# A graph network of two layers on one core: epsilon and offset of the layer norms and the mask of unlinked nodes go to VectorE, and every operation gets a new place

## The chip, the core and the metric

The kernel runs on one core of a Trainium2 chip. A core has five engines that each work through their own queue in order: TensorE (PE) for matrix products, VectorE (DVE), ScalarE (ACT), GpSimd (POOL), and SyncE (SP), which here only issues transfers between HBM and the on-chip memory SBUF. Products land in banks of a second on-chip memory, PSUM. The metric is device time in microseconds (us) of one execution, the median of several.

## The reference, cut to what matters

The input is 64 graphs of 256 nodes with 256 features each, and for each graph a 256 x 256 matrix `adj` of links, here 0 or 1. Two layers follow each other:

```python
# layer 0: attention with 8 heads of 32 features; values differ by the kind of link
attn = softmax(q @ k.T / sqrt(32))                      # q = x@Wq+bq, k = x@Wk+bk, per head
out  = sum_r (attn * (adj == r)) @ (x @ Wv[r] + bv[r])  # with links 0 and 1: r = 0, 1
x    = ln(x + out @ Wo + bo, g1, beta1)                 # norm 1
x    = ln(x + gelu(x @ W1 + b1) @ W2 + b2, g2, beta2)   # norm 2; 256 -> 1024 -> 256
# layer 1: two graph-attention steps, then a second feed-forward
def gat(h, W, a):
    Wh = h @ W
    e  = leaky_relu(Wh @ a[:256] + (Wh @ a[256:]).T, 0.2)
    return softmax(where(adj > 0, e, -9e15), axis=1) @ Wh
h = ln(x + gat(gat(x, W1, a1), W2, a2), g_ln1, b_ln1)            # norm 3
h = ln(h + relu(h @ w_ff1 + b_ff1) @ w_ff2 + b_ff2, g_ln2, b_ln2)  # norm 4
# ln(x) = (x - mean) * rsqrt(var + 1e-5) * g + b
```

So each graph has four layer norms, and the mask of the unlinked nodes is used twice, once in each graph-attention step.

## The kernel before, in words

`binary_graphs` writes one program for all 64 graphs. (A second function, `any_graphs`, serves links above 1; with this input it does no work.) Of a graph, the 256 nodes are two blocks of 128 partitions. All arithmetic is float32 except the links, which are bfloat16 once they have been transposed (`adT`).

**The stages of a graph, with the names of their operations.** The letters and digits stand for themselves below: a name like `bc1` is one operation of the plan.

- *Front.* `load` brings features and links, `cast` (GpSimd) makes the links bfloat16 and their transpose follows by a transfer, `xT` (VectorE) transposes the features, `xS` (GpSimd) makes sums of their blocks. `no` (L552) makes the mask of unlinked nodes from `adT`: 1 where a link is <= 0, 128x512, as unsigned bytes, on GpSimd.
- *Attention.* Two halves m = 0, 1 of four heads: `qk` (L558) and its copy `qkc`; the scores `s` (L606), whose matmuls use tiles of 32 rows; then per head VectorE's `max`, ScalarE's `exp`, VectorE's `rec` (the reciprocal of the sums), ScalarE's `nrm`, VectorE's `eT` (a transpose within squares of 32), a write to DRAM and a read back (`eW`, `eR`) that finish the transpose, and VectorE's `pm` (L638), the masked copy. `vp1` to `vp7` (L582) are the seven products of the values, for both kinds of link at once, `va` (L591) and `vb` their sums. `po` (L653) is the sum over both masks, with output tiles of 32 columns; ScalarE's `oT` (L659) copies it, `wo` (L673) projects it, `ya` adds the residual.
- *Feed-forward, twice* (prefix `a` and `b` in names; `ffa`, `ffb` in the rows): `T`, `W`, `R` transpose the input through DRAM, `t1` to `t4` (GpSimd) make differences of its blocks, `p1` to `p7` (L455) are the seven products of the way up, in the order 1, 2, 6, 7, 5, 4, 3 or near it, where 1, 6, 7 and 4 are accumulated in one and the same PSUM bank: between them ScalarE's copies `c1`, `c6`, `c7`, `c4` (L466) take the intermediate state out, and the next product waits for that copy. `a1`, `a7`, `a6` (VectorE, L472) add two further banks. `x0` to `x3` are the activation, `S1` to `S4` (GpSimd, L492) differences, `d1` to `d7` (L503) the seven products of the way down, `e` the additions to the residual.
- *Graph attention*: `ga` and `gac`; for steps A and B `ip`, `z`, `zl`, the masking `zm` (L708, VectorE's predicated copy of -9e15 where `no` is nonzero), `zx`, `ze`, `zd`; `h1` and `h1c`; `h2` (L745) and `h2a`.
- *Norm n of 1 to 4* (class `Norm`): `st` (VectorE: mean and variance, into `mv`), `rt` (GpSimd, L387 and L388: variance plus epsilon, then the power -1/2, into `rs`), `nb` (GpSimd, L392 and L393: mean times `rs`, then times -1), `ln` (ScalarE, L398, two instructions that apply scale `rs` and offset `nb`). After norms 2 and 4 GpSimd multiplies the gain (`lg`) and adds the shift (`lb`).

**What sets the order.** Nothing is reordered by a compiler. A table `PLACES` gives each of these operations a place in time; the operation of graph g is sorted by `g * PERIOD + place`, with a `PERIOD` of 46.802, and all operations of all graphs are written in that order. Since a graph's places spread over more than six periods, some six graphs are in flight, and between two projections `wo` on TensorE stand products of several graphs. An engine's own queue is that order, cut down to its instructions. An instruction waits for its inputs by semaphores, and everything behind it in its queue waits with it.

Four kinds of things come once and are sorted in by places of their own: 49 late loads of weights (`LOAD_PLACES`, issued by SyncE, L864), and the preparations of the values' weights, the output bias, the two feed-forwards and the graph attention (`V_PLACE`, `OUT_PLACE`, `FFA_PLACE`, `FFB_PLACE`, `GAT_PLACE`). Some first loads and graph 0's input stand ahead of everything.

**Orders that the change touches.** The queues of one period, from one projection to the next, as the places of the kernel before sort them:

```
TensorE: wo vp7 s0 qk1 vp2 bp1 bp2 bp6 vp5 vp3 bp7 bp5 bp4 bp3 ga1 ga0 s1 vp4 ipA bd1 ap1 ap2 bd5 ap6 ...
         ... bd4 bd3 po0 ad3 ad5 ad7 ad1 ad2 ad4 h2 vp1 ad6 qk0 vp6 po1
ScalarE: ln2 nrm13 nrm10 ln4 nrm11 exp02 qkc1 bc1 ln1 bc6 exp01 bc7 ... exp10 nrm01 nrm12 te ln3 qkc0 oT1
```

Rings of buffers: three PSUM banks for most products (`mm`), one bank for each of the four heads' scores, one for `po`; three buffers for `no`, six for each small tensor of the norms.

## Time and profile before

| | us |
|---|---|
| median of three runs | 3115.67 (3115.14 to 3116.3) |
| profiled execution, whole | 3118.7 |
| its span, first to last instruction | 3116.9 |
| mean granted TensorE clock | 0.987 of full speed |
| GpSimd, power of the norms, L388 | 713 ns, 256 times |
| ScalarE, application of the norms, L398 | 595 ns, 256 times |
| VectorE, reciprocal of the heads' sums, L624 | 149 ns a piece from 1000 to 2872 us |
| VectorE, masked copy `pm`, L638 | 899 ns, 512 times |

The profile comes from one execution with its own time, so durations are read against the span of that execution and not against the median. A row of a group gives the line of the kernel, the engine, the operation, the output and inputs by their names and shapes, how often it ran, its summed and mean time, and the idle time of the engine just ahead of it with the instruction that ended it. In timelines a row is the start, the length, the engine and the line, and several instructions of one kind in a row are one row. TensorE's lengths overlap a little, because matmuls are pipelined: a start is surer than an end.

### The profile page before, as it was taken

To read this page: it belongs to the slowest core of one execution; us is meant where nothing else is said; L and a number is where in the kernel's file an instruction comes from. 1 tells how busy PE (TensorE), PEld (TensorE's weight loads), DVE (VectorE), ACT (ScalarE), POOL (GpSimd) and SP (SyncE) were. 2 spreads that over 40 slices of the span, in tenths; PEclk is the share of its full clock that TensorE was granted. 3 is DMA by queue.
4 is the path that set the end of the run, shared out by engine and by line. 5 is a ranking of instruction groups with operands and counts; after the bars stand their busy time and mean duration, and the time that the engine had idled before them with its cause. 6 is when DMAs were issued, how large, how long until landed. Compare 5 with 4: busy or idle time off the path is not lost.

```text
span 3116.9 us, 72178 instructions
## 1 busy us (share of the span) xinstructions
PE 3020.8 (97%) x24797; PEld 2611.0 (84%) x24797; DVE 2618.7 (84%) x5545; ACT 2597.0 (83%) x7109; POOL 2364.2 (76%) x3142
## 2 busy tenths in 40 slices
PE   6899999999999999999999999999999999999985
PEld 4688888888888888888888888888888888888874
DVE  6888888888888888888888888888888888888852
ACT  5688888888888888888888888888888888888852
POOL 1577777877877877877877877877878777787763
PEclk8899999999999999999999999999999999999997
DMA  7554555455455455455455455455455555445410
GB/s 188 163 158 144 145 162 151 144 160 152 142 157 161 136 160 161 137 157 155 135 160 156 140 156 154 142 154 158 145 147 159 146 146 162 147 143 162 143 50 27
DMA packets 808371, 457.16 MB, mean 147 GB/s; under 512 B 334529, under 2 KB 717377, under 8 KB 808001
## 3 DMA queue, kind: packets, MB, share of 16 engines
q1 hardware_dynamic: 808000, 452.49, 50.3%
q8 instruction: 200, 3.28, 0.5%
q14 instruction: 171, 1.39, 0.1%
HBM read 242.63 MB, written 201.33 MB: 142 GB/s over the span
## 4 chain that ended last, share of the span: by engine, by line
PE 93%; DMA 2%; DVE 2%; ACT 2%; POOL 1%; issue 1%; SPq 0%; POOLq 0%; DVEq 0%; ACTq 0%
PE ffb_ps L455 14%; PE ffa_ps L455 13%; PE ffb_po L503 7%; PE po L653 7%; PE qk_ps L558 7%; PE ffa_po L503 7%; PE v_ps L582 6%; PE ffa_pq L503 6%; PE ffb_pq L503 5%; PE s L606 4%; PE wo_ps L673 4%; PE h_ps L730 4%; PE h_ps L745 3%; PE ga_wps L683 3%; DMA ffa_T<-ffa_T_d 1%
## 5 line engine op out<-in xcount | busy, mean ns | idle before, releaser
L619 ACT ACTIVATE e<-s,nmax 128x256 f32<-128x256 f32 x1024 | 473.6, 476 | 10.6 <-DVE nmax L611 10.4
L629 ACT ACTIVATE e<-e,rden 128x256 f32<-128x256 f32 x1024 | 447.6, 502 | 25.0 <-DVE rden L624 25.0
L638 DVE TENSOR_TENSOR pm<-eT,adT 128x512 f32<-128x512 f32 x512 | 449.5, 899 | 0.0
L340 DVE STREAM_TRANSPOSE eT_sq<-e 128x512 f32<-128x512 f32 x512 | 349.1, 691 | 7.3 <-ACT e L629 6.0
L611 DVE TENSOR_REDUCE nmax<-s 128x2 f32<-128x512 f32 x512 | 341.7, 669 | 2.0 <-PE s L606 2.0
L478 ACT ACTIVATE ffb_h<-ffb_h,bf_c 128x256 f32<-128x256 f32 x512 | 224.9, 503 | 49.0 <-DVE ffb_h L472 49.0
L492 POOL TENSOR_TENSOR ffb_t<-ffb_h 128x512 f32<-128x512 f32 x64 | 81.5, 1273 | 225.8 <-ACT ffb_h L478 225.8
L466 ACT COPY ffb_h<-ffb_ps 128x512 f32<-128x512 f32 x256 | 151.0, 590 | 99.6 <-PE ffb_ps L455 99.5
L472 DVE TENSOR_TENSOR ffb_h<-ffb_ps,ffb_h 128x512 f32<-128x512 f32 x192 | 132.8, 692 | 107.2 <-PE ffb_ps L455 104.2
L466 ACT COPY ffa_h<-ffa_ps 128x512 f32<-128x512 f32 x256 | 148.3, 579 | 83.5 <-PE ffa_ps L455 47.8
L492 POOL TENSOR_TENSOR ffa_t<-ffa_h 128x512 f32<-128x512 f32 x64 | 82.5, 1289 | 172.6 <-PE ffb_pq L503 155.0
L619 ACT ACTIVATION_READ_ACCUMULATOR e<-s,nmax 128x1 f32 x1024 | 211.5, 207 | 0.0
L478 ACT ACTIVATE ffa_h<-ffa_h,b_c 128x256 f32<-128x256 f32 x512 | 211.1, 506 | 0.1
L472 DVE TENSOR_TENSOR ffa_h<-ffa_ps,ffa_h 128x512 f32<-128x512 f32 x192 | 132.3, 689 | 79.7 <-ACT ffa_h L466 45.8
L388 POOL TENSOR_TENSOR rs_x<-rs_x,nhalf 128x2 f32<-128x2 f32 x256 | 182.5, 713 | 21.3
L492 POOL TENSOR_TENSOR ffb_t<-ffb_h,ffb_t 128x512 f32<-128x512 f32 x128 | 163.6, 1278 | 36.3 <-ACT ffb_h L478 35.6
L492 POOL TENSOR_TENSOR ffa_t<-ffa_h,ffa_t 128x512 f32<-128x512 f32 x128 | 185.0, 1445 | 5.0
L591 DVE TENSOR_TENSOR v<-v,v_ps 128x256 f32<-128x256 f32 x448 | 177.2, 407 | 2.0 <-PE v_ps L582 1.1
L398 ACT ACTIVATE ffa_res<-ffa_res,nb_x,rs_x 128x256 f32<-128x256 f32 x256 | 139.9, 595 | 25.2 <-POOL nb_x L393 24.8
L455 PE MATMUL ffb_ps<-ffb_T,f 128*128 128x128 f32 x1024 | 130.7, 283 | 26.7 <-DMA ffb_T<-ffb_T_d 22.9
L606 PE MATMUL s<-kT,qT 32*128 32x256 f32 x2048 | 149.8, 407 | 7.0 <-ACT e L619 6.0
L558 PE MATMUL qk_ps<-xT,wq 128*128 128x256 f32 x512 | 141.1, 399 | 15.9 <-DVE xT L529 8.4
(192 smaller groups left out, 9799.1 us busy)
## 6 DMA issues: line engine op xcount, KB each, us to landing
eT_d<-eT_sq SPq DMA_DIRECT2D x512, 256.0 KB, 3.1
eT<-eT_d SPq DMA_DIRECT2D x512, 256.0 KB, 3.6
xin<-in_x_dram SPq DMA_DIRECT2D x256, 64.0 KB, 3.6
adi<-in_adj_dram SPq DMA_DIRECT2D x64, 256.0 KB, 2.6
y<-in_x_dram SPq DMA_DIRECT2D x64, 256.0 KB, 2.9
ffa_T_d<-ffa_T_sq SPq DMA_DIRECT2D x64, 256.0 KB, 2.8
ffa_T<-ffa_T_d SPq DMA_DIRECT2D x64, 256.0 KB, 2.9
hT_d<-hT_sq SPq DMA_DIRECT2D x64, 256.0 KB, 2.1
```

Of the source, the lines that this page charges most:

```text
L340: nc.vector.transpose(self.sq.rearrange("p a c k y -> p (c k) a y"), src.rearrange("p c (k a x) -> p (c k) a x", k=KD, a=A))
L455: nc.tensor.matmul(self.ps[bank][:, f], w[:, f * P:(f + 1) * P], b, start=(i in (1, 2, 5) and f == 0), stop=(f == KF // 2 - 1), skip_group ...
L466: nc.scalar.copy(self.half_of(*{1: (0, 0), 6: (0, 1), 7: (1, 1), 4: (1, 0)}[i]), self.ps[0])
L478: nc.scalar.activation(h, h, self.func, bias=self.ba[:, f0 + f:f0 + f + 1])
L492: nc.gpsimd.tensor_tensor(out, a, b, ALU.subtract)
L503: nc.tensor.matmul(self.p[bank][:, k], a[:, f], seven[self.name[:3]][i][:, f], start=(f == 0), stop=(f == KF // 2 - 1))
L558: nc.tensor.matmul(p[:, i, :], w[:, k, m * P:(m + 1) * P], self.xT[:, k, :], start=(k == 0), stop=(k == KD - 1))
L606: nc.tensor.matmul(self.s4[m][h][:, ic * N:(ic + 1) * N], self.qT[hp, m, ic * P:(ic + 1) * P], self.kT[hp, m, :], start=True, stop=True)
L611: nc.vector.tensor_reduce(self.nmax[m, h], self.s4[m][h].rearrange("p (c n) -> p c n", c=C), AX.X, ALU.max, negate=True)
L619: nc.scalar.activation(e[:, ic, :], self.s4[m][h][:, ic * N:(ic + 1) * N], AF.Exp, bias=self.nmax[m, h][:, ic:ic + 1], accum_out=self.den[ ...
L629: nc.scalar.activation(e[:, ic, :], e[:, ic, :], AF.Copy, scale=self.rden[m, h][:, ic:ic + 1])
L638: nc.vector.tensor_tensor(self.pm[m, h].rearrange("p c k (b y) -> p (c k) b y", b=A), t.rearrange("p b c k y -> p (c k) b y"), self.adT.re ...
```

## The change

Three pieces of code differ, and the table of places as a whole.

1. In the norms, the addition of epsilon becomes an operation of its own, `ep`, made by VectorE; `rt` keeps only the power on GpSimd. The offset `nb`, two GpSimd instructions before, becomes a single VectorE instruction that computes (mean * -1) * `rs`. There are so four new operations `ep1` to `ep4` in the plan.
2. The mask `no` is made by VectorE, and as bfloat16 (two bytes) in place of bytes. The predicated copies read it as 16-bit integers: bfloat16 1.0 is a nonzero integer, 0.0 is zero.
3. All places of `PLACES` and `LOAD_PLACES` and five of the six single places are new. `PERIOD`, the rings of buffers and all other instructions stay.

The orders of one period as the new places sort them, in the parts quoted above:

```
TensorE: wo qk0 qk1 vp7 s0 bp1 bp2 bp6 vp5 vp3 bp7 bp5 bp4 bp3 ga0 ga1 vp4 s1 ipA bd1 ap1 bd5 ap2 ap6 ...
         ... bd4 bd3 po0 ad2 ad5 ad3 ad1 ad7 ad4 h2 vp1 vp6 ad6 po1 vp2
ScalarE: nrm10 ln2 nrm12 qkc0 ln4 nrm13 qkc1 ln1 bc1 exp00 bc6 nrm11 bc7 ... exp10 exp11 te ln3 oT1
```

The diff, with the tables of places cut to lines that hold the operations named in the prediction:

```diff
@@ PLACES @@
-    "nrm00": 164.2327, "jT": 164.3427, "max12": 165.7236, "eT00": 167.5746, "exp12": 169.7100, "exp13": 170.5568,
...
-    "vp7": 179.5750, "nrm10": 181.4170, "eT12": 181.4243, "va6": 181.4250, "pm02": 181.5909, "nrm11": 181.7985,
-    "eW01": 181.9127, "va7": 182.2184, "eW12": 183.4518, "eT10": 183.7174, "vp2": 184.3903, "va1": 185.0411,
...
-    "eR01": 203.3696, "eR12": 205.4702, "vb0": 206.0359, "pm01": 206.6006, "eR11": 208.3873, "no": 208.5428,
...
-    "pm11": 218.7878, "yb": 220.5903, "po1": 224.1269, "oT1": 224.3347, "wo": 224.5498, "ya": 228.6368,
-    "st1": 229.0414, "rt1": 229.1629, "nb1": 230.6009, "ln1": 234.3259, "aT": 234.4225, "aW": 240.6669,
...
-    "st2": 270.8686, "rt2": 271.2157, "nb2": 271.6584, "ln2": 272.2136, "lg2": 273.5284, "lb2": 275.9453,
...
-    "zdB": 310.2557, "h2": 313.2543, "h2a": 313.6724, "st3": 314.2692, "rt3": 314.7577, "nb3": 315.5806,
-    "ln3": 317.6585, "bT": 318.1117, "bW": 320.1436, "bR": 322.7256, "bp1": 325.4569, "bp2": 325.4761,
-    "bt1": 325.6400, "bc1": 326.5166, "ba1": 327.5467, "bt2": 327.9860, "bp6": 328.1851, "bc6": 329.1500,
...
+    "vc1": 173.9536, "exp10": 174.3248, "vp6": 174.5314, "exp11": 175.3003, "vp2": 175.8095, "rec12": 176.1291,
...
+    "y": 198.1955, "eT11": 203.0863, "eW11": 203.8664, "no": 205.1910, "eR13": 205.6991, "vb0": 207.9039,
...
+    "pm12": 219.2104, "po1": 222.4051, "yb": 222.9595, "oT1": 224.5787, "wo": 224.6869, "ya": 226.7172,
+    "st1": 227.1616, "ep1": 227.4558, "rt1": 229.3943, "nb1": 230.0763, "ln1": 233.0766, "aT": 233.5465,
...
+    "ae6": 270.0682, "st2": 270.5735, "ep2": 271.7058, "rt2": 272.0693, "nb2": 272.1488, "ln2": 273.4515,
...
+    "ep3": 316.6501, "rt3": 316.8392, "nb3": 317.0634, "ln3": 318.0361, "bT": 318.3054, "bW": 320.1997,
...
+    "bc1": 327.4034, "ba1": 328.4472, "bp6": 328.5483, "bc6": 328.7027, "bt4": 329.5370, "bp7": 330.4200,
...
+    "ep4": 359.3714, "rt4": 360.5104, "nb4": 367.5449, "ln4": 371.4297, "lg4": 378.3959, "lb4": 379.2432,
@@ LOAD_PLACES @@
-    105.247, 106.338, 251.305, 142.756, 226.120, 202.518, 180.231, 135.528, 193.356, 105.689, 128.568, 205.544,
...
+    144.047, 142.557, 27.397, 25.047, 27.401, 116.952, 116.957, 27.393, 43.262, 29.713, 131.552, 28.533, -6.038,
...
-V_PLACE, OUT_PLACE, FFA_PLACE, GAT_PLACE, FFB_PLACE, ODD_PLACE = 135.857, 138.353, 239.224, 193.799, 285.406, 240.000
+V_PLACE, OUT_PLACE, FFA_PLACE, GAT_PLACE, FFB_PLACE, ODD_PLACE = 27.390, 204.579, 160.180, 258.716, 208.569, 240.000
@@ class Norm @@
+        def shifted(self):
+            self.rs = small.tile([P, C], F32, tag="rs", name=f"rs_{self.name}")
+            nc.vector.tensor_scalar(self.rs, self.mv[:, :, 1], EPS, None, op0=ALU.add)
+
         def root(self):
-            self.rs = small.tile([P, C], F32, tag="rs", name=f"rs_{self.name}")
-            nc.gpsimd.tensor_scalar(self.rs, self.mv[:, :, 1], EPS, None, op0=ALU.add)
             nc.gpsimd.tensor_tensor(self.rs, self.rs, nhalf, ALU.pow)
 
         def offset(self):
             self.nb = small.tile([P, C], F32, tag="nb", name=f"nb_{self.name}")
-            nc.gpsimd.tensor_tensor(self.nb, self.mv[:, :, 0], self.rs, ALU.mult)
-            nc.gpsimd.tensor_scalar(self.nb, self.nb, -1.0, None, op0=ALU.mult)
+            nc.vector.scalar_tensor_tensor(self.nb, self.mv[:, :, 0], -1.0, self.rs, op0=ALU.mult, op1=ALU.mult)
@@ class Graph @@
         def unlinked(self):
-            self.no = fp.tile([P, C, C, P], U8, tag="no", name=f"no{self.g}", bufs=3)
-            nc.gpsimd.tensor_scalar(self.no, self.adT, 0.0, None, op0=ALU.is_le)
+            self.no = fp.tile([P, C, C, P], BF16, tag="no", name=f"no{self.g}", bufs=3)
+            nc.vector.tensor_scalar(self.no, self.adT, 0.0, None, op0=ALU.is_le)
...
         def gat_mask(self):
-            nc.vector.copy_predicated(self.z.rearrange("p c (i n) -> p i c n", i=C), self.no, negc[:, :, None, None].to_broadcast([P, C, C, P]))
+            nc.vector.copy_predicated(self.z.rearrange("p c (i n) -> p i c n", i=C), self.no.bitcast(mybir.dt.uint16), negc[:, :, None, None].to_broadcast([P, C, C, P]))
...
                 ops[f"st{n}"] = lambda norm=norm, src=src: norm.stats(src())
+                ops[f"ep{n}"] = norm.shifted
```

## The prediction, written before the changed kernel ran

> **What bounds the kernel now.** I read the page's head first, then the table of stretches, then TensorE's timeline over one repetition, then the groups of GpSimd and VectorE, last the chain near the start. The page's first lines and the stretches (columns: start:end, length, busy time and instructions of PE, weight load, VectorE, ScalarE, GpSimd, then granted clock, DMA share, GB/s):
>
> ```profile
> PE 3020.8 (97%) x24797; PEld 2611.0 (84%) x24797; DVE 2618.7 (84%) x5545; ACT 2597.0 (83%) x7109; POOL 2364.2 (76%) x3142
> ```
> ```profile
> 0.00:100.00 100.00, 67.11 (x442) 49.76 (x442) 67.39 (x140) 57.41 (x172) 28.74 (x43) 0.88 0.73 196
> ...
> 1000.00:2000.00 1000.00, 997.45 (x8292) 866.14 (x8292) 869.00 (x1842) 868.81 (x2384) 791.65 (x1046) 1.00 0.53 152
> ...
> 3000.00:3117.00 117.00, 73.40 (x480) 65.27 (x479) 37.59 (x79) 44.69 (x108) 53.23 (x68) 0.83 0.09 26
> ```
>
> TensorE is never idle in the middle; it is idle at both ends only. VectorE is at 87% in the middle, GpSimd at 79%. So a graph costs what TensorE's queue costs, and an edit on another engine counts only where TensorE then waits more or less. TensorE's timeline (start, length) over one output projection of the graph before and the stretch up to the next:
>
> ```profile
> 2850.38 2.08 PE L673 MATMUL wo_ps<-wo,oT 128*128 128x256 f32 x8
> ...
> 2889.49 1.89 PE L745 MATMUL h_ps<-gb_wh,gb_z 128*128 128x256 f32 x8
> 2891.22 0.59 PE L582 MATMUL v_ps<-wv,xT 128*128 128x256 f32 x2
> ...
> 2895.70 1.05 PE L653 MATMUL po<-pm,v 128*32 128x256 f32 x16
> 2896.72 2.07 PE L673 MATMUL wo_ps<-wo,oT 128*128 128x256 f32 x8
> 2898.63 0.59 PE L582 MATMUL v_ps<-wv,xs 128*128 128x256 f32 x2
> ```
>
> From one projection to the next is 2896.72 - 2850.38 = 46.34 us, the cost of a graph. 64 x 46.34 = 2965.8; the other 151.1 us of the span are filling and draining, and some waits of a few us between.
>
> The same rows show waits that the busy share hides, because a matmul that waits briefly overlaps the one before. Eight 256-column matmuls take 1.73 us to the next group in the second attention layer (2889.49 to 2891.22), but 1.91 in the output projection (2896.72 to 2898.63). Leaving the 32-column tiles of `po` costs about 0.11 of that: elsewhere in this timeline a group of eight 128-column matmuls takes 1.00 behind `po` and 0.89 otherwise. The other 0.07, and 0.04 more ahead of the projection (1.02 against 0.98 from the masked half of `po` to what follows it there), is the wait for ScalarE's copy of `po1` (0.37 us) that the projection reads: 0.11 us a graph.
>
> **The change part by part.** GpSimd's and VectorE's groups from 1000 to 2872 us, 40 graphs (count | busy, mean ns | idle before), with the one small VectorE `TENSOR_SCALAR` of the start:
>
> ```profile
> L388 POOL TENSOR_TENSOR rs_x<-rs_x,nhalf 128x2 f32<-128x2 f32 x160 | 114.1, 713 | 13.3
> L552 POOL TENSOR_SCALAR no<-adT 128x512 uint8<-128x512 bf16 x40 | 61.3, 1532 | 0.0
> L393 POOL TENSOR_SCALAR nb_x<-nb_x 128x2 f32<-128x2 f32 x160 | 36.7, 229 | 14.0
> L387 POOL TENSOR_SCALAR rs_x<-mv_x 128x2 f32<-128x2 f32 x160 | 35.3, 220 | 28.6 <-DVE mv_x L383 18.8
> L392 POOL TENSOR_TENSOR nb_x<-mv_x,rs_x 128x2 f32<-128x2 f32 x160 | 31.2, 195 | 9.4
> ```
> ```profile
> L624 DVE RECIPROCAL rden<-den 128x2 f32<-128x2 f32 x323 | 41.4, 149 | 0.0
> ...
> L708 DVE COPY_PREDICATED_SCALAR ga_z<-no,negc 128x512 f32 x41 | 32.6, 796 | 1.4
> ...
> L215 DVE TENSOR_SCALAR bqs_c<-bq_c 128x2 f32<-128x2 f32 x1 | 0.5, 468 | 1.8 <-DMA bq_c<-in_L_gnn_bq_dram 1.8
> ```
>
> GpSimd loses, per graph, 4 x (0.220 + 0.195 + 0.229) + 1.532 = 4.11 us; it falls from 79% to 70%. None of it was waited for by TensorE in the middle, so this is worth nothing by itself.
>
> VectorE gains four epsilon additions, four offsets and the mask. A small one is taken at 0.149, the reciprocal of the same shape (ends: 0.060, a memset of 128x2 at the start, and the 0.468 above). The mask, 128x512 bfloat16 in and out, has no near row; VectorE's 128x512 float32 instructions take 0.67 to 0.69. The Trainium skill (VectorE: DVE Perf Modes, The perf-mode tier table) lets a bfloat16 `tensor_scalar` in SBUF run at four elements a cycle; with that page's fixed 150 cycles an estimate is (150 + 512/4)/0.96 = 0.29. I take 0.29, and 0.69 as the other end. Sum: 8 x 0.149 + 0.29 = 1.48 us a graph, VectorE from 87% to 90.5%. Cover: its remaining 4 us of idle time a graph. The two predicated copies read a mask twice as wide; 0.796 each is kept (0.67 to 1.06 are the ends, the lower one the other 128x512 rows, the upper a third more), and they lie beside TensorE's `po` and feed-forward products.
>
> Here a rule speaks against the change. In the middle `pm` takes 0.68 alone, but:
>
> ```profile
> 2838.52 2.96 POOL L492 TENSOR_TENSOR ffa_t<-ffa_h,ffa_t 128x512 f32<-128x512 f32 x2
> ...
> 2838.59 1.75 DVE L638 TENSOR_TENSOR pm<-eT,adT 128x512 f32<-128x512 f32 x1
> ```
>
> The Trainium skill (SBUF — State Buffer, Who interferes with whom) says that a VectorE instruction with two SBUF inputs, or in a two-port mode, and a GpSimd instruction that reads SBUF exclude each other for a whole instruction. The row agrees: `pm` lost 1.07 us. All nine new instructions are of those kinds. By the rule, each meeting a busy GpSimd (0.70) and waiting half of a 1.28 us instruction, they add 9 x 0.70 x 0.64 = 4.0 us a graph: VectorE at 45.9 of 46.34 us, no longer under cover. By the rows alone 1.48. The order decides between them: behind the `pow` of norms 1 and 2 GpSimd next waits for a landing (`bt1` for its read) or for the norm itself (`lg2` for `ln2`), so their offsets find it idle; offset 3 meets the cast (0.61), the epsilons and the mask meet anything. I take five exposed, 5 x 0.45 = 2.2, so about 44.1 us, 95%: covered, barely.
>
> Waits added: each offset waits on VectorE for the `pow` on GpSimd. `ae5` and `ae6` (0.4 + 0.54) stand between for norm 3, a v addition and a transpose (0.38 + 0.69) for norm 2, `pm02`, `hT` and a transpose (2.0) for norm 1, nearly a repetition for norm 4, against 0.71 and two handovers of 0.1. Queued behind offset 3 are a reciprocal and the statistics of norm 2, behind offset 1 a v addition and the maxima that ScalarE's exponentials wait for.
>
> Places. TensorE's order per graph keeps the four stretches of 32-wide tiles (two of scores, two of `po`) and their switching costs, and the filling between the feed-forward products and their copies. What differs: `vp2` (0.43) now stands between `po1` and the projection. It covers the copy's remainder of 0.11: -0.11 x 64 = -7.0 us. The cost without it is that 0.11.
>
> Norm chain: in the timeline of GpSimd statistics end at 2854.46 and the offset at 2856.24, 1.78 us; after it is 0.15 + 0.1 + 0.71 + 0.1 + 0.15 = 1.21. In the middle this is hidden behind TensorE. The last graph has its four norms end to end: 4 x 0.57 = -2.3.
>
> Start. In the SyncE queue 29 of the 49 late loads stand ahead of graph 1's input, 15 before:
>
> ```profile
> 12.80 7.86 DMA w<-in_L_gnn_W_dram
> ...
> 24.03 3.45 DMA xin<-in_x_dram
> ...
> 119.77 0.70 DVE ffb_u L262
> ```
>
> 14 more issues of about 0.62 put that input, graph 0's transposes and their reads, which queue behind it, 8.7 us later; TensorE waited 5.85 there already. Against it, the second feed-forward's weight preparation, whose VectorE chain from 119.04 to 127.16 made TensorE wait 5.57 and cost it 4.75 for the bias product, moves ahead of the first `po`, where TensorE starves anyway; the first one's moves forward too. The attention weights' preparation moves back into loaded time (its stalls: 2.85 + 0.78). 8.7 + 3.6 - 10.3 = +2.0, bounds -8 and +10; I take 0, as graph 0's three early norms give back 1.7.
>
> Sum: 3116.9 - 7.0 - 2.3 = 3107.6. The profiled run took 3118.7, 1.8 more than its span; the median of the three runs shown, 3115.67, is 1.2 under the span. So 3107.6 - 1.2 = 3106.4 us.
>
> **The rivals.** (A) The above. (B) The time stays within 0.2%, which is about what a measurement of this kernel can tell from no change: the copy of `po1` now stands behind `ln3` on ScalarE, whose offset ends just then, so the wait stays and is only renamed; or the start takes back 7 us. 3115.7.
>
> (C) Slower: `ln1` now stands ahead of the first copy of the second feed-forward (`bc1`) on ScalarE, it stood behind. From the projection's start TensorE needs 1.73 + two `qk` of 1.74 + 0.43 + 1.18 for scores + 1.0 to fill the bank, so the copy could start at 8.05. ScalarE has by then `oT` 0.37, a normalising 0.89, `ln2` 1.08, and only after it come GpSimd's gain and shift (2.64), then `hT`, a transpose and the offset on VectorE (1.6), `ln1` 1.09: 7.7. Spare: 0.35. ScalarE's own backlog between (4.7) puts it at 8.1. If VectorE's exclusion makes it x later than that, TensorE waits x in each graph; the gain of A is gone at 0.14 and slower by 0.2% is reached at (3121.9 - 3106.4)/64 = 0.24. At half an exclusion above it, x = 0.5: 3138. For it: the rule above; against: VectorE's 5% of spare time and the 0.35.
>
> That the mask would cost the same on VectorE as on GpSimd doesn't matter while covered.
>
> **How the numbers follow.** A 0.42, B 0.20, C 0.38. A alone runs from 3096 (start at its better bound) to 3109.4. The whole range goes from 3096 into C, to x = 0.56: 3142; I leave out 0.04 below and 0.14 above. Faster 0.42, same 0.20, slower 0.38.
>
> **What would show it.** A: the eight matmuls of the projection take 1.73 to the next group (1.84 if they stand right behind 32-wide tiles), a graph takes 46.23, GpSimd is at 70% in the middle, VectorE at 90 to 95%. B: a graph at 46.3 with a wait named ScalarE ahead of the projection, or the start later. C: a graph above 46.5, with waits of `ffb_ps` for ScalarE's copy and `y` normalised late. Wrong altogether: VectorE at 98%, or the first matmul of graph 1 more than 10 us later without the later gain.

## The result and the profile after

The changed kernel takes 3185.07 us (median of six runs, 3183.82 to 3186.62) where the kernel before took 3115.99 beside it: a ratio of 1.0214, interval 1.0201 to 1.0227. It is slower by 69 us, 43 us above the upper end of the predicted range.

Engines and stretches first: the line of busy times from the page of the changed kernel, then its stretch from 1000 to 2000 us (length, busy time and instructions of PE, weight load, VectorE, ScalarE, GpSimd, then clock, DMA share, GB/s).

```profile
PE 3042.7 (96%) x24797; PEld 2635.6 (83%) x24797; DVE 2822.2 (89%) x6121; ACT 2600.4 (82%) x7109; POOL 2104.7 (66%) x2310
```
```profile
1000.00:2000.00 1000.00, 984.30 (x8145) 855.70 (x8144) 924.36 (x2005) 854.59 (x2341) 694.18 (x760) 1.00 0.51 148
```

In the middle VectorE went from 87% to 92% and GpSimd from 79% to 69%, as the prediction had it. TensorE, at full clock (1.00), did 8145 matmuls in this millisecond where it did 8292 in the kernel before. From one projection to the next (the median over the run, from the starts of L674) a graph now takes 47.29 us, 46.34 before.

The difference of the spans, 3184.8 - 3116.9 = 67.9 us, divides by the starts of the projections: up to the third one 171.05 against 157.39, +13.7; from there to the last, 61 graphs, 2885.6 against 2829.9, +55.7; behind the last 128.1 against 129.6, -1.5.

Where TensorE waits in a graph is in its timeline (start, length, and in brackets the idle time ahead and what ended it):

```profile
2010.36 1.89 PE L746 MATMUL h_ps<-gb_wh,gb_z 128*128 128x256 f32 x8
...
2015.80 0.70 PE L583 MATMUL v_ps<-wv,xT 128*128 128x256 f32 x2
2016.98 1.99 PE L674 MATMUL wo_ps<-wo,oT 128*128 128x256 f32 x8 [0.48 <-ACT oT L660]
2018.81 1.03 PE L559 MATMUL qk_ps<-xT,wq 128*128 128x256 f32 x4
...
2023.86 2.11 PE L456 MATMUL ffb_ps<-ffb_T,f 128*128 128x128 f32 x16
2026.17 1.13 PE L456 MATMUL ffb_ps<-ffb_xt,ffb_u 128*128 128x128 f32 x8 [0.20 <-ACT ffb_h L467]
```

The brackets count only time in which nothing runs; from start to start the loss is larger. `vp2` starts at 2015.80 and needs 0.43; the projection starts 1.18 later, so 0.75 us are lost in front of it. The sixteen matmuls of p1 and p2 (`bp1` and `bp2`) need 1.79; p6 (`bp6`) starts 2.31 later, 0.5 lost where 0.04 was lost before. Both recur in every graph (over 40 of them 0.75 and 0.51 in the mean).

Of each loss about 0.11 is no wait but the price of leaving narrower tiles, which the kernel before paid at another place: where the projection waits for nothing (run 10 below) it starts 0.54 behind `vp2`, and the shortest distance from p1 to p6 in 39 graphs here is 1.90. That leaves 0.64 of waiting ahead of the projection, 0.04 before, and 0.42 ahead of p6, 0.03 before. Behind the projection the next group starts after 1.83, 1.91 before; 1.73 was forecast, and run 10 has 1.73. So a projection that had to wait costs 0.1 more behind it too.

Both waits end with ScalarE, but neither begins there. The chain can be followed on VectorE, ScalarE and GpSimd, same kernel, one timeline each:

```profile
2012.28 0.69 DVE L750 TENSOR_TENSOR ffa_res<-h_ps,ffa_res 128x512 f32<-128x512 f32 x1
...
2014.01 0.17 DVE L387 TENSOR_SCALAR rs_x<-mv_x 128x2 f32<-128x2 f32 x1
2014.09 1.01 DVE L512 TENSOR_TENSOR ffa_res<-ffa_po,ffa_res 128x256 f32<-128x256 f32 x2
2015.02 0.52 DVE L394 SCALAR_TENSOR_TENSOR nb_x<-mv_x,rs_x 128x2 f32<-128x2 f32 x1
...
2016.19 0.29 DVE L383 BATCH_NORM_AGGREGATE mv_x<-st_x 128x2 f32<-128x6 f32 x2
2016.70 0.71 DVE L340 STREAM_TRANSPOSE ffb_T_sq<-ffa_res 128x512 f32<-128x512 f32 x1 [0.22 <-ACT ffa_res L399]
2017.34 0.13 DVE L387 TENSOR_SCALAR rs_x<-mv_x 128x2 f32<-128x2 f32 x1
```
```profile
2015.58 1.09 ACT L399 ACTIVATE ffa_res<-ffa_res,nb_x,rs_x 128x256 f32<-128x256 f32 x2 [0.50 <-DVE nb_x L394]
2016.57 0.35 ACT L660 COPY oT<-po 128x256 f32<-128x256 f32 x1
...
2024.47 1.09 ACT L399 ACTIVATE y<-y,nb_x,rs_x 128x256 f32<-128x256 f32 x2 [0.39 <-DVE nb_x L394]
2025.46 0.56 ACT L467 COPY ffb_h<-ffb_ps 128x512 f32<-128x512 f32 x1
```
```profile
2019.66 1.27 POOL L365 TENSOR_TENSOR ffa_res<-ffa_res,g_r 128x512 f32<-128x512 f32 x1 [1.42 <-ACT ffa_res L399]
2021.01 1.27 POOL L368 TENSOR_TENSOR ffa_res<-ffa_res,be_r 128x512 f32<-128x512 f32 x1
2022.38 1.07 POOL L390 TENSOR_TENSOR rs_x<-rs_x,nhalf 128x2 f32<-128x2 f32 x1
```

`h2` is added by `h2a` at 2012.28; then come the statistics, `ep3` at 2014.01, the power, offset 3 at 2015.02 (0.52 long), `ln3` at 2015.58, and only behind `ln3` the copy `oT1` that the projection reads. `ln3` also leads on: to the transpose `bT`, behind which norm 2's epsilon stands (its statistics end at 2016.48, it starts at 2017.34), to `ln2` (2018.48 to 2019.58), its gain and shift on GpSimd, and only behind these norm 1's power at 2022.38, offset 1 at 2024.04, `ln1` at 2024.47, and behind `ln1` the copy `bc1` that p6 waits for. So three norms of three different graphs stand in one chain from `h2` to p6, tied together by the order of the queues. Measured on TensorE from the start of `h2` to the start of p6, and from there to the next `h2` (medians of 39 graphs):

| kernel | h2 to p6 | p6 to the next h2 | a graph |
|---|---|---|---|
| before | 14.82 | 31.52 | 46.34 |
| changed | 15.82 | 31.47 | 47.29 |

The whole difference lies in the first stretch, a third of the period, and the growth of the two waits, 0.60 and 0.39, makes up all of it. Yet the two norms on whose ends TensorE waits, 3 and 1, come no later in it than before. The same stretch in ScalarE's timeline of the kernel before, where `h2` starts at 2008.42:

```profile
2013.78 1.09 ACT L398 ACTIVATE ffa_res<-ffa_res,nb_x,rs_x 128x256 f32<-128x256 f32 x2
...
2015.73 0.37 ACT L659 COPY oT<-po 128x256 f32<-128x256 f32 x1
...
2022.51 0.59 ACT L466 COPY ffb_h<-ffb_ps 128x512 f32<-128x512 f32 x1 [0.37 <-PE ffb_ps L455]
2022.99 1.09 ACT L398 ACTIVATE y<-y,nb_x,rs_x 128x256 f32<-128x256 f32 x2
```

Starts behind that of `h2`, in us (medians of 40 graphs; "run 1" has the new places with the old engines, "run 9" the changed kernel with a shorter offset 3, see below):

| | before | changed | run 1 | run 9 |
|---|---|---|---|---|
| `ln3` | 5.37 | 5.22 | 5.37 | 4.85 |
| last matmul of `po1` | 6.87 | 5.13 | 5.13 | 5.13 |
| projection | 7.23 | 6.62 | 6.77 | 6.25 |
| `ln2` | 7.59 | 8.13 | 7.63 | 7.76 |
| `ln1` | 14.58 | 14.12 | 13.75 | 13.74 |
| `bc1` | 14.10 | 15.12 | 14.85 | 14.73 |

In the kernel before `oT1` stood behind `ln3` too, but `ln3` was over before `po1` was done, and `bc1` stood ahead of `ln1`. In the changed kernel `po1` is done 1.74 earlier, since the product `qk0` went behind the projection, while `ln3` comes as it did; and `bc1` has to wait for `ln1`. TensorE now waits at two points for a chain that it did not wait for before.

What the small instructions cost now (groups of VectorE from 1000 to 2872 us: count | busy, mean ns | idle before):

```profile
L387 DVE TENSOR_SCALAR rs_x<-mv_x 128x2 f32<-128x2 f32 x159 | 78.8, 496 | 2.7
L394 DVE SCALAR_TENSOR_TENSOR nb_x<-mv_x,rs_x 128x2 f32<-128x2 f32 x159 | 77.3, 486 | 0.0
...
L625 DVE RECIPROCAL rden<-den 128x2 f32<-128x2 f32 x318 | 47.6, 150 | 0.0
...
L709 DVE COPY_PREDICATED_SCALAR gb_z<-no,negc 128x512 f32 x40 | 31.9, 798 | 1.4
...
L553 DVE TENSOR_SCALAR no<-adT 128x512 bf16<-128x512 bf16 x40 | 10.3, 258 | 0.0
```

Epsilon and offset take 0.49 us, not 0.149; the mask takes 0.258 and the copies that read it are as fast as before. The nine instructions come to 4 x (0.496 + 0.486) + 0.258 = 4.19 us a graph.

### The profile page after: what moved, and what is told of

Same layout as the page of the kernel before. It is cut to its first block, busy times and chain, and to the rows that moved or that the text cites. A ratio compares the mean times of both kernels' runs of the same rounds, so it can differ in the third digit from the quotient of the medians.

```text
span 3184.8 us, 71412 instructions
## 1 busy us (share of the span) xinstructions
PE 3042.7 (96%) x24797; PEld 2635.6 (83%) x24797; DVE 2822.2 (89%) x6121; ACT 2600.4 (82%) x7109; POOL 2104.7 (66%) x2310
## 4 chain that ended last, share of the span: by engine, by line
PE 64%; DVE 22%; ACT 6%; issue 4%; DMA 2%; SPq 1%; POOL 1%; DVEq 0%; POOLq 0%; ACTq 0%
PE ffa_ps L456 13%; PE ffb_ps L456 10%; PE ffb_po L504 7%; PE ffa_pq L504 6%; PE ffb_pq L504 5%; DVE ffa_res L512 5%; PE ffa_po L504 5%; PE po L654 4%; PE h_ps L731 3%; PE ga_wps L684 3%; DVE nb_x L394 3%; DVE st_x L381 3%; PE v_ps L583 3%; PE s L607 2%; ACT ffa_res L399 2%
## 5 line engine op out<-in xcount | busy, mean ns | idle before, releaser
L630 ACT ACTIVATE e<-e,rden 128x256 f32<-128x256 f32 x1024 | 462.8, 503 | 4.9 <-DVE rden L625 4.9
L639 DVE TENSOR_TENSOR pm<-eT,adT 128x512 f32<-128x512 f32 x512 | 415.9, 834 | 5.7 <-DMA eT<-eT_d 5.7
L390 POOL TENSOR_TENSOR rs_x<-rs_x,nhalf 128x2 f32<-128x2 f32 x256 | 225.0, 879 | 235.6 <-DVE rs_x L387 222.7
L493 POOL TENSOR_TENSOR ffb_t<-ffb_h 128x512 f32<-128x512 f32 x64 | 81.3, 1270 | 300.6 <-ACT ffb_h L479 300.6
L493 POOL TENSOR_TENSOR ffa_t<-ffa_h 128x512 f32<-128x512 f32 x64 | 82.6, 1290 | 284.6 <-PE ffb_pq L504 259.5
L473 DVE TENSOR_TENSOR ffa_h<-ffa_ps,ffa_h 128x512 f32<-128x512 f32 x192 | 132.8, 692 | 103.4 <-PE ffa_ps L456 84.5
L493 POOL TENSOR_TENSOR ffa_t<-ffa_h,ffa_t 128x512 f32<-128x512 f32 x128 | 210.6, 1645 | 5.0
L592 DVE TENSOR_TENSOR v<-v,v_ps 128x256 f32<-128x256 f32 x448 | 177.9, 409 | 23.0 <-PE v_ps L583 22.9
L493 POOL TENSOR_TENSOR ffb_t<-ffb_h,ffb_t 128x512 f32<-128x512 f32 x128 | 163.9, 1281 | 22.4 <-ACT ffb_h L479 22.0
L473 DVE TENSOR_TENSOR ffb_h<-ffb_ps,ffb_h 128x512 f32<-128x512 f32 x192 | 129.9, 677 | 52.7 <-PE ffb_ps L456 52.7
L595 ACT COPY v<-v_ps 128x256 f32<-128x256 f32 x64 | 23.9, 373 | 176.9 <-PE v_ps L583 174.3
L456 PEld LDWEIGHTS ffb_ps<-ffb_T,f 128*128 128x128 f32 x1024 | 127.7, 198 | 46.6 <-issue 42.5
L456 PE MATMUL ffb_ps<-ffb_T,f 128*128 128x128 f32 x1024 | 140.1, 292 | 25.2 <-DMA ffb_T<-ffb_T_d 22.2
```

The lines of the kernel that those rows point to most:

```text
L390: nc.gpsimd.tensor_tensor(self.rs, self.rs, nhalf, ALU.pow)
L456: nc.tensor.matmul(self.ps[bank][:, f], w[:, f * P:(f + 1) * P], b, start=(i in (1, 2, 5) and f == 0), stop=(f == KF // 2 - 1), skip_group ...
L473: nc.vector.tensor_tensor(t, self.ps[bank], t, ALU.add)
L493: nc.gpsimd.tensor_tensor(out, a, b, ALU.subtract)
L630: nc.scalar.activation(e[:, ic, :], e[:, ic, :], AF.Copy, scale=self.rden[m, h][:, ic:ic + 1])
L639: nc.vector.tensor_tensor(self.pm[m, h].rearrange("p c k (b y) -> p (c k) b y", b=A), t.rearrange("p b c k y -> p (c k) b y"), self.adT.re ...
```

## The experiments

Each time is compared with runs of the kernel before on the same chip. A "graph" is the median distance of two projections; numbers of lines are those of the kernel in question; losses ahead of the projection and of p6 are counted from start to start as above, the 0.11 included. Theory O: the new order of the queues costs the time. Theory E: the move of the instructions to VectorE costs it. E has two forms. W: an offset at the head of VectorE's queue waits there for GpSimd's power, and what stands behind it waits too. X: VectorE and GpSimd exclude each other, so that each of the moved instructions gets longer.

**1. The new places alone.**

```diff
 # changed kernel, its places
-            nc.vector.tensor_scalar(self.rs, self.mv[:, :, 1], EPS, None, op0=ALU.add)   # ep
+            nc.gpsimd.tensor_scalar(self.rs, self.mv[:, :, 1], EPS, None, op0=ALU.add)   # in rt
-            nc.vector.scalar_tensor_tensor(self.nb, ...)
+            nc.gpsimd.tensor_tensor(self.nb, ...); nc.gpsimd.tensor_scalar(self.nb, ...)
-            self.no: BF16, nc.vector
+            self.no: U8, nc.gpsimd
```

> The changed kernel's places, with everything that went to VectorE made by GpSimd again as in the kernel before (epsilon together with the power, the offset in two instructions, the mask as bytes). Theory O (the order costs: the copy oT1 stands behind ln3 and bc1 behind ln1 on ScalarE, and each of these is late whatever engine makes the offset): the wait ahead of the projection stays, since statistics at 6.98 in the changed kernel's timeline, then 0.22 + 0.71 + 0.20 + 0.23 and handovers on GpSimd put ln3 at 8.54 against 8.58 now; the wait for bc1 shrinks, because norm 1's offset is no longer delayed: a graph at about 46.8, 3145 to 3165 us. Theory E (the engines cost: nine overlong VectorE instructions): both waits are gone, a graph at 46.2 to 46.4, 3115 to 3130 us with the later start.

3170.35 us, ratio 1.0163 (1.0146 to 1.0180); a graph 47.04, h2 to p6 15.58. The loss ahead of the projection is 0.89, the one ahead of p6 nearly gone (0.14). So O's waits are as expected, a little larger (the time is 5 us above O's upper end), and the new order costs 0.70 us a graph even with the old engines. The start is late here too: first projection at 80.4, third at 172.3.

**2. The engines alone.**

```diff
 # changed kernel's engines
-PLACES, LOAD_PLACES and single places of the changed kernel
+those of the kernel before; "ep1".."ep4" = "st1".."st4" + 0.0001
```

> The places of the kernel before (loads and preparations too), with epsilon (right behind the statistics), offset and mask made by VectorE as in the changed kernel. Theory O: bc1 stands ahead of ln1 again and st3 comes 2 us earlier in the period, so the longer VectorE instructions find slack: a graph at 46.34 to 46.5, 3112 to 3128 us. Theory E: VectorE is at 92% and late, a graph above 47, 3160 to 3190 us.

3199.64 us, ratio 1.0263 (1.0246 to 1.0281): slower than the changed kernel itself and 10 us above E's upper end. A graph 47.64, h2 to p6 16.19; the first projection at 61.0, as early as before. So the engines cost 1.29 us a graph in the old order, and only 47.29 - 47.04 = 0.25 in the new one: of the changed kernel's 0.95 us a graph the order accounts for 0.70. Neither theory holds alone, and E not in its form of nine equal instructions, as the next runs show.

**3. and 4. The pairs on ScalarE that the two waits name.** In the changed kernel, in 3 `bc1` goes ahead of `ln1`; in 4 also `oT1` ahead of `ln3`.

```diff
-"bc1": 327.4034
+"bc1": 326.6796
 # and in 4:
-"oT1": 224.5787
+"oT1": 224.4311
```

> The changed kernel with one pair exchanged on ScalarE: bc1 right ahead of ln1 instead of behind it. Theory O, from the trace: the 0.47 us that TensorE waits for bc1 ahead of the product p6 go, the 0.75 ahead of the projection stay: a graph at 46.8, 3150 to 3160 us. Theory E: norm 1 is as late as before and its delay shows at the first feed-forward instead (its products p1 wait for the transpose): a graph at 47.2 to 47.3, 3178 to 3187 us.

> The changed kernel with two pairs exchanged on ScalarE: bc1 ahead of ln1, and oT1 ahead of ln3. Theory O: both waits go, 47.29 - 0.47 - 0.65 = 46.2 us a graph; the later start (about 14 us) stays: 3112 to 3125 us. Theory E: VectorE is the bound and the waits turn up elsewhere: a graph above 46.8, over 3150 us.

Neither theory's numbers came: 3210.84 us (1.0293, 1.0276 to 1.0310; a graph 47.68) and 3200.17 us (1.0259, 1.0242 to 1.0276; 47.47). From TensorE's timelines, of 3 and of 4:

```profile
2036.54 1.99 PE L674 MATMUL wo_ps<-wo,oT 128*128 128x256 f32 x8 [0.48 <-ACT oT L660]
...
2047.57 0.70 PE L583 MATMUL v_ps<-wv_t,xT 128*128 128x256 f32 x2 [0.66 <-DVE ffb_h L473]
```
```profile
2036.41 1.16 PE L456 MATMUL ffb_ps<-ffb_T,f 128*128 128x128 f32 x8 [0.66 <-DVE v L592]
```

In 3 the wait for `bc1` went and another came: `ln1` now stands behind `bc1`, for which ScalarE waits 0.99 until TensorE has its product; VectorE waits 1.30 for `ln1` ahead of the transpose `aT`, and behind that stands the addition (L473) that empties a PSUM bank. That wait lies behind p6: h2 to p6 is 15.45 in this run, and the rest of the period, 31.4 to 31.5 in the other kernels, is 32.23. In 4 the wait ahead of the projection went and p2 waits for a bank that a value addition (L592) empties, which stands behind offset 1. In both runs TensorE met the end of a norm again, at another place.

**5. to 7. One part of the engines' move at a time, in the old places.** Only the mask; only the epsilons, right behind the statistics; only the offsets. The other lines are those of the kernel before.

```diff
 # 5
-            nc.gpsimd.tensor_scalar(self.no, self.adT, 0.0, None, op0=ALU.is_le)   # U8
+            nc.vector.tensor_scalar(self.no, self.adT, 0.0, None, op0=ALU.is_le)   # BF16, read as 16-bit integers
 # 6
-            nc.gpsimd.tensor_scalar(self.rs, self.mv[:, :, 1], EPS, None, op0=ALU.add)   # in rt
+            nc.vector.tensor_scalar(self.rs, self.mv[:, :, 1], EPS, None, op0=ALU.add)   # ep
 # 7
-            nc.gpsimd.tensor_tensor(self.nb, ...); nc.gpsimd.tensor_scalar(self.nb, ...)
+            nc.vector.scalar_tensor_tensor(self.nb, ...)
```

> The kernel before, with only the mask made by VectorE as bfloat16 and read as 16-bit integers; norms on GpSimd as before, all places as before. Its 0.26 us stands far from the waits that the trace of the engines alone shows. Theory W (VectorE's in-order wait for the power, ahead of each offset, holds back what is queued behind it): nothing, a graph at 46.34 to 46.4, 3113 to 3122 us. Theory X (the nine new instructions cost by exclusion with GpSimd, each about alike): about a ninth of the 1.29 us that the engines alone cost, 46.5, 3125 to 3130 us.

> The kernel before, with only the epsilon additions made by VectorE, right behind the statistics; offsets and mask on GpSimd, all places as before. VectorE waits for nobody in them. Theory W: little, a graph at 46.34 to 46.55, 3113 to 3130 us. Theory X: epsilon took 0.496 us on VectorE in the changed kernel, the offset 0.486, so about half of the 1.29 us: a graph at 46.9 to 47.0, 3150 to 3160 us.

> The kernel before, with only the offsets made by VectorE in one instruction, which waits there for GpSimd's power; epsilon and mask on GpSimd, all places as before. Theory W: nearly all of the 1.29 us, and the trace has VectorE idle ahead of L394, released by GpSimd: a graph at 47.2 to 47.6, 3170 to 3195 us. Theory X: half, 46.9 to 47.0, 3150 to 3160 us.

| only | us | ratio (interval) | a graph | h2 to p6 |
|---|---|---|---|---|
| mask | 3122.42 | 1.0007 (0.9998 to 1.0016) | 46.35 | 14.83 |
| epsilons | 3145.35 | 1.0081 (1.0064 to 1.0097) | 46.78 | 15.34 |
| offsets | 3175.57 | 1.0174 (1.0157 to 1.0191) | 47.21 | 15.71 |

The mask costs nothing that shows, as W and the prediction had it (the time is 0.4 us above W's upper end). The offsets cost 0.87, two thirds of the engines' 1.29, and the epsilons the rest, 0.44: more than W left them, less than X gave them. The run of the offsets alone shows what W says, in its groups and on VectorE's and ScalarE's timelines:

```profile
L396 DVE SCALAR_TENSOR_TENSOR nb_x<-mv_x,rs_x 128x2 f32<-128x2 f32 x160 | 37.3, 233 | 45.4 <-POOL rs_x L392 45.4
```
```profile
2001.13 0.30 DVE L384 BATCH_NORM_AGGREGATE mv_x<-st_x 128x2 f32<-128x6 f32 x2
2002.56 0.16 DVE L396 SCALAR_TENSOR_TENSOR nb_x<-mv_x,rs_x 128x2 f32<-128x2 f32 x1 [1.13 <-POOL rs_x L392]
2002.64 0.42 DVE L514 TENSOR_TENSOR ffa_res<-ffa_po,ffa_res 128x256 f32<-128x256 f32 x1
2002.97 0.22 DVE L627 RECIPROCAL rden<-den 128x2 f32<-128x2 f32 x2
```
```profile
2003.22 0.91 ACT L632 ACTIVATE e<-e,rden 128x256 f32<-128x256 f32 x2 [0.92 <-DVE rden L627]
2004.04 0.19 ACT L756 ACTIVATE spare<-nhalf 128x1 f32<-128x1 f32 x1
2004.13 1.08 ACT L401 ACTIVATE ffa_res<-ffa_res,nb_x,rs_x 128x256 f32<-128x256 f32 x2
```

Offset 3 takes 0.16, but VectorE stands still 1.13 ahead of it, waiting for the power. Behind it in the queue are two reciprocals; ScalarE waits 0.92 for them, and behind that stand `ln3`, `qkc0` and `oT1`. TensorE loses 1.0 us ahead of the projection.

**8. The offset of norm 3 out of the way.** The run of the offsets alone with one place changed.

```diff
-"nb3": 315.5806
+"nb3": 316.4520     # behind rec12, rec11 and ae6, ahead of st2
```

> The kernel before with only the offsets on VectorE (as in the run that moved the offsets alone), and one place changed: the offset of norm 3 stands behind the two reciprocals and the two feed-forward additions that it held back, 0.3 us ahead of the next statistics, so that GpSimd's power is done by then. Theory W (the in-order wait for the power is the cost): the 1.0 us that TensorE waits ahead of the projection go, a graph at 46.34 to 46.5, 3113 to 3130 us. If the offsets cost in another way (exclusion, their own time): above 46.9, over 3150 us.

3116.70 us beside 3121.20 before: ratio 0.9989 (0.9980 to 0.9998), a graph 46.35. VectorE's idle time ahead of the offsets falls from 45.4 to 9.3 us:

```profile
L396 DVE SCALAR_TENSOR_TENSOR nb_x<-mv_x,rs_x 128x2 f32<-128x2 f32 x160 | 35.7, 244 | 9.3 <-POOL rs_x L392 9.3
```

W holds for the offsets in the old order: one place takes back all of the 0.87 us. This kernel is also the only one here with an interval below 1, by a tenth of a per cent.

**9. The exclusion on the chain, in the changed kernel.** In its timeline offset 3 (2015.02) takes 0.52, and GpSimd starts the cast of the links (0.61) at 2014.91. The cast is put ahead of norm 3's power.

```diff
-"cast": 130.6264
+"cast": 129.6112
```

> The changed kernel with one place changed: on GpSimd the cast of the links stands ahead of norm 3's power instead of behind its offset's place, so that VectorE's offset 3 no longer meets it. Theory X on the chain (the exclusion makes offset 3 0.52 us instead of 0.12, and the chain of norms 3, 2, 1 sets the period): 0.4 us less a graph, 46.9, 3155 to 3165 us. If the chain is set elsewhere: 47.2 to 47.3, 3178 to 3187 us.

3162.04 us, ratio 1.0135 (1.0119 to 1.0152), against 1.0214: a graph 46.90, h2 to p6 15.44, the loss ahead of the projection 0.38 in place of 0.75. The groups of VectorE:

```profile
L394 DVE SCALAR_TENSOR_TENSOR nb_x<-mv_x,rs_x 128x2 f32<-128x2 f32 x160 | 62.2, 389 | 0.0
```

The offsets' mean falls by about 0.1, which is 0.4 for one of four, and the period falls by 0.39. `ln3`, the projection, `ln2`, `ln1` and `bc1` all come 0.37 to 0.39 earlier behind `h2` (last column of the table above), so the chain is the one that sets the period. An exclusion of 0.4 us of a 128x2 instruction is paid in full because it lies on that chain: in the new order it is X that works, where VectorE never idles ahead of an offset.

**10. Is the wait local?** `qk0` goes back ahead of `po1`, its copy ahead of `oT1`.

```diff
-"qk0": 133.0638   "qkc0": 135.4937
+"qk0": 128.7911   "qkc0": 130.9647
```

> The changed kernel with the product qk0 moved back ahead of po1 on TensorE and its copy ahead of that of po1 on ScalarE, as in the kernel before: 1.73 us of TensorE work more between h2 and the projection, as much less behind it. If the wait ahead of the projection is local (too little work in front of it): it goes, 0.75 us a graph, 46.5 to 46.6, 3135 to 3145 us. If the chain from h2 through norms 3, 2 and 1 to the copy bc1 sets the period (15.8 us from h2 to p6 in the changed kernel, 14.8 before, while the rest of the period is 31.5 in both): the wait turns up ahead of p6, a graph stays at 47.2 to 47.4, 3178 to 3190 us.

3204.28 us (1.0267, 1.0250 to 1.0284; a graph 47.53), 14 us above the upper end for the chain and on its side. The timeline of TensorE has the wait ahead of p6:

```profile
2043.41 1.13 PE L456 MATMUL ffb_ps<-ffb_xt,ffb_u 128*128 128x128 f32 x8 [1.26 <-ACT ffb_h L467]
```

More work ahead of the projection doesn't shorten the chain; it moved the wait and, with another copy on ScalarE ahead of `oT1`, lengthened the chain by 0.25 (h2 to p6 16.07).

**11. The prediction's gain by itself.** The kernel before with `vp2` between `po1` and the projection; and **12.** the same on top of run 8, with the addition that empties `vp2`'s bank moved forward.

```diff
-"vp2": 184.3903
+"vp2": 177.6978
 # and in 12, with run 8's kernel:
-"va1": 185.0411
+"va1": 181.5000     # right behind va6
```

> The kernel before with one place changed: the value product vp2 stands on TensorE between po1 and the projection, as in the changed kernel. Step A of the prediction: it covers the 0.11 us of waiting for the copy of po1: a graph at 46.23, 7 us less than before (3108 to 3113 us beside 3118). If that 0.11 comes back at another wait of the same stretch (the chain of norms up to the product p6): a graph at 46.34, within 2 us of before.

> The kernel before with the offsets on VectorE and three places changed: the offset of norm 3 late (as in the run with the late offset), vp2 between po1 and the projection, and the addition va1 that releases vp2's bank right behind va6 instead of 3.6 us later. In the run with vp2 alone the second half of the products p1 and p2 waited 0.43 us for that bank. If the bank was the only cost, the 0.11 us are had: a graph at 46.23, 5 to 8 us less than the late offset alone. If 0.4 us more on VectorE ahead of the residual's addition costs as much in the chain: 46.34 or more, no gain.

3155.48 us (1.0121, 1.0104 to 1.0137; a graph 46.93), far above both expectations, and 3155.08 us (1.0111, 1.0094 to 1.0128; 46.95), on the side of no gain. The timelines of TensorE, of 11 and of 12:

```profile
2045.09 1.05 PE L455 MATMUL ffb_ps<-ffb_T,f 128*128 128x128 f32 x8
2046.57 1.16 PE L455 MATMUL ffb_ps<-ffb_T,f 128*128 128x128 f32 x8 [0.43 <-DVE v L591]
```
```profile
2051.80 1.13 PE L458 MATMUL ffb_ps<-ffb_xt,ffb_u 128*128 128x128 f32 x8 [0.48 <-POOL ffb_xt L443]
```

In 11 the product issued earlier holds one of the three PSUM banks of the ring until its addition, and p2 waits for that bank. In 12 the bank is released early; but the addition's 0.4 us stand ahead of the residual's on VectorE, and the masked copy between them meets GpSimd's gain and shift (1.60 in this graph, 0.68 in the kernel before); the chain to norm 1 is later, GpSimd's differences too, and p6 waits for these. The 0.11 us couldn't be had in either way: `vp2` in this place costs 0.6 us a graph.

**13. Loads and preparations.** The changed kernel with `LOAD_PLACES` and the single places of the kernel before.

```diff
-LOAD_PLACES and V_, OUT_, FFA_, GAT_, FFB_PLACE of the changed kernel
+those of the kernel before
```

> The changed kernel with the places of the late loads and of the weights' preparations of the kernel before; the order of the graphs' operations and the engines as changed. If these places make the start later, the first projection is back near 62 us from 80.5, a graph stays at 47.29, and the whole is about 14 us shorter: 3167 to 3175 us. If the later start comes from the order of graph 0's own operations: 3182 to 3188 us.

3182.35 us, ratio 1.0200 (1.0183 to 1.0217). The first projection comes at 68.3 in place of 80.5, but the third at 170.1 against 171.1: the 12 us are lost again. So the places of the loads and preparations delay the first projection, but they are not what delays the third. The later start is in run 1 and not in run 2, so it is not the engines either; it comes with the order of the graphs' operations. Which of them is not settled.

**14. and 15. What the epsilons cost.** In 14 all three moves in the old places with `nb3` as in run 8; in 15 the epsilons alone with `ep4` behind the two masked copies instead of ahead of them.

```diff
 # 14, from run 2
-"nb3": 315.5806
+"nb3": 316.4520
 # 15, from run 6
-"ep4": 358.2378
+"ep4": 359.2537
```

> All three moves to VectorE in the places of the kernel before (as in the run of the engines alone), with the offset of norm 3 behind the reciprocals and additions that it held back. Theory W plus the epsilons' own cost: the engines alone cost 1.29 us a graph, of which the wait of offset 3 is 0.85 and the epsilons 0.44; so a graph at 46.78, 3142 to 3150 us. If the parts are not additive (the mask and epsilons also cost through that wait): below 46.5 or above 47.0.

> The kernel before with only the epsilons on VectorE (as in the run that moved these alone), norm 4's one place later: behind the two masked copies instead of ahead of them. In the trace of the epsilons alone these copies end 0.24 us later, the additions behind them release their bank as much later, and the product ad6 waits 0.23 us for it. If that position is the cost: 0.2 less a graph, 46.55 to 46.6, 3128 to 3135 us. If any 0.17 us more on VectorE in this stretch costs the same: 46.75 to 46.8, 3142 to 3148 us.

14: 3138.90 us (1.0059, 1.0042 to 1.0076), a graph 46.71 where 46.78 was expected; the parts add up to within 0.07. 15: 3136.24 us (1.0051, 1.0034 to 1.0068), a graph 46.60, as the position has it: 0.18 of the 0.44 were `ep4` ahead of the masked copies. In run 6 VectorE's timeline has it so:

```profile
2025.37 0.17 DVE L388 TENSOR_SCALAR rs_x<-mv_x 128x2 f32<-128x2 f32 x1
2025.45 1.86 DVE L641 TENSOR_TENSOR pm<-eT,adT 128x512 f32<-128x512 f32 x2
2027.23 0.55 DVE L514 TENSOR_TENSOR ffa_res<-ffa_pq,ffa_res 128x384 f32<-128x384 f32 x1
```

In the kernel before the same two copies took 1.54. Counted from the aggregation of the statistics they start 0.20 later than there and take 0.32 longer beside GpSimd, and the additions behind them, which had waited for a product, start 0.35 later. The remaining 0.26 us of the epsilons were not taken apart. Two more things stay open: which of the new places makes the order's 0.70 us was read from traces and not isolated, and no run puts `qk0` back ahead of the projection and `bc1` ahead of `ln1` together, as both stood before.

## Why the prediction was wrong

**The bound was read rightly: TensorE's queue costs a graph, and its waits count. Two steps failed, the first of them the larger.**

**A, the gain of 7.0 us: `vp2` "covers the copy's remainder of 0.11".** It took the wait for the copy of `po1` to be the time of that copy, which in the kernel before it was: there the copy starts as soon as `po1` is done. It didn't ask what else the copy waits for once `qk0` (1.73) has left the place ahead of it. The last matmul of `po1` then starts 5.13 behind `h2`, but `ln3` only 5.22, a microsecond long and with the copy behind it; so the wait grew from 0.04 to 0.64. With the old engines the new places alone cost 0.70 us a graph (run 1), where the step had -0.11. Rival B named `ln3` but priced it at the old wait; and "now stands behind `ln3`" is not the change, for the copy stood behind `ln3` in the old order too. Runs 11 and 12 show that `vp2` between `po1` and the projection is no gain in the old order either.

**"Cover: its remaining 4 us of idle time a graph".** VectorE's idle time lies elsewhere in the period: of 5.8 us a graph in the kernel before 4.4 lie between p6 and the next `h2`, 1.4 between `h2` and p6. In the new order the chain of three norms runs through this stretch and sets the period, and what is added to it is paid: the engines cost 0.25 us a graph on top of the places, and 0.39 go when one offset meets no cast (run 9).

**The price of the small instructions was nearly right and decided nothing.** Undisturbed the row of 0.149 holds: over the 40 graphs 80 epsilons that met no GpSimd instruction took 0.148 in the mean, 41 offsets 0.119. But 40 epsilons with one of L493 in flight took 1.24, 39 with one of L368 0.45; 40 offsets with L365 took 0.93, 40 with the cast 0.52, 37 with the differences of L441 0.39. That is five of nine exposed, as the prediction took it, at 0.57 each in place of 0.45; 4.19 us in place of 3.7. The count is partly luck: offset 1, which was to find GpSimd idle, met the differences, and the mask came through at its own 0.258 in 39 of 40 graphs. VectorE is busy for 0.924 x 47.29 = 43.7 us of a graph, 44.1 were forecast; the masked copies `pm` got shorter meanwhile, 839 ns in the mean for 896. The rule of the Trainium skill (SBUF — State Buffer, Who interferes with whom) agrees with these rows; the prediction's estimate from it, each of the nine exposed by GpSimd's busy share, gave 5.5 us: too much, on the right side. What failed is the conclusion drawn from the sum, "covered, barely".

**The waits added.** "Queued behind offset 3 are a reciprocal and the statistics of norm 2" named the mechanism and gave it no price. In the old order it is 0.87 us a graph (runs 7 and 8). In the new order the offsets' waits are in fact filled, as the prediction said: VectorE is idle 0.0 ahead of L394. But an epsilon waits: norm 2's stands behind the transpose that waits for `ln3`, and `ln2` comes 8.13 behind `h2`, 7.63 with the epsilon on GpSimd and the same places (run 1).

**C** was right in place, direction and nearly in size: 0.39 more of waiting ahead of p6, where 0.5 was its example. The terms of its first sum add up to 7.82, not 8.05, so by its own numbers the spare was 0.12 and not 0.35; in the changed kernel the copy starts 8.50 behind the projection's start. And C stood for this wait alone. With the 0.60 more ahead of the projection it makes the 1.00 us from `h2` to p6; the rest of the period is 0.05 shorter. Of 0.95 us a graph 55.7 us remain over 61 graphs, because both runs have a few irregular graphs.

**Start and tail.** The tail gave 1.5 for the 2.3 forecast. The start cost 13.7, outside the bounds of -8 and +10; its working by loads fits the first projection, but run 13 shows that the third is as late without the new loads. (The better bound, -8, gives 3098.4 for A's lower end; 3096 was written. Nothing hangs on it.)

**What held:** the mask (0.258 for 0.29, nothing in the end), the predicated copies (0.80), GpSimd at 69% and VectorE at 92%, and that GpSimd's relief is worth nothing by itself.

## What to carry to other kernels

Where every queue is in order, look for the stretch of the period in which a chain of dependent work is as long as the work of the engine that bounds the kernel, and price an edit there at full length, however idle the edited engine is over the period. Such a chain shows as soon as work leaves the bounding engine in that stretch, though the chain itself is no slower; a wait on TensorE is only where the chain touches it, and in runs 3, 4 and 10 mending one such place moved the wait to another. A small instruction moved to another engine brings its wait along: put it behind the work that it would hold back, not where its input is nominally ready. A duration that depends on what a neighbour has in flight is a property of the place: read it there.

## What the runs showed that was not expected

A VectorE instruction on 128x2 took between 0.12 and 1.24 us, by what GpSimd did; the reciprocal of the same shape took 0.15 in the mean whether GpSimd was busy (238 of them) or idle (80). GpSimd's power on 128x2 in turn went from 0.71 to 0.88 in the mean: 1.07 where VectorE's masked copy (L639, both inputs in SBUF) ran beside it (79 of them, 2022.38 above is one), 0.70 beside additions that read PSUM (L512 and L592, 80). The one that starts first is hardly held: a mask that starts at 2044.80 takes its usual 0.26 and GpSimd's addition (L368), which starts at 2044.85, 1.34 in place of 1.27; in the one graph of 40 where such an addition had started 0.90 earlier, the mask took 0.53.
